# Three blocks of deformable samples gathered ahead inside the attention stage instead of two

## The chip, the cores and the metric

The kernel is one program for one NeuronCore of a Trainium2 chip; it uses one core. Time is the device time of one execution in microseconds (us). The core has five engines that each work through an instruction stream of their own, in order: TensorE (PE, matrix products and transposes), VectorE (DVE), ScalarE (ACT), GpSimd (POOL) and SyncE (SP), which here only issues transfers. Transfers run on 16 DMA engines that all queues share. The result of a transfer or an instruction is handed on by a semaphore, and an instruction that waits holds everything behind it on its engine.

## The reference, cut to what matters

The reference takes two images of 256 channels and 64 x 64 pixels through four layers:

```
x = group_norm(x) + proj(attention(group_norm(x)))      # 4 heads, 4096 x 4096 scores per head
x = x + position_term                                    # linear in the pixel's place
x = relu(x + bn(conv1x1(relu(bn(dcn(relu(bn(conv1x1(x))))))))   # bottleneck, 64 channels inside
h = relu(group_norm(x));  h = deform_conv(h, ...1)       # first deformable layer
h = relu(group_norm(h));  h = deform_conv(h, ...2)       # second
out = h + x
```

In each deformable convolution (the bottleneck's `dcn` too) every output pixel has nine taps, and every tap samples the image at a computed place: the four pixels around that place are read and weighted. In the last layer the places come from `off`: a depthwise 7 x 7 convolution followed by a 1 x 1 to 18 channels. All of it is float32.

## The kernel before, in words

**Two stages.** `attention` (line 181) computes the attention of both images, and between its steps it carries, as background work, the bottleneck of image 0 and the first part of the bottleneck of image 1. `deform` (line 1319) then runs four layers: first deformable layer of images 0 and 1, second of images 0 and 1, with image 1's bottleneck convolution beside the first of them. The order of the instructions on PE, ACT, DVE and POOL is the order in which the Python loops write them; only SP's order is chosen by the framework, which also places all the semaphores. So each loop counter below is a place in the program that can be counted without a chip.

**Attention's loop** counts score tiles with `n`, from 0 to 1024, two at a time (a pair). 256 tiles are a unit (one image, two heads), 16 tiles are a `Block` of 256 queries. A tile is 128 queries by 1024 keys: products on PE (L580), the row's largest value on DVE (L592), exponentials on ACT (L598), 16 transposes on PE (L610) that ACT and DVE copy back (L629, L627), products with the values (L639). At a block's end DVE copies the product into the one tile `o` (L471), the softmax's denominators go to DRAM and come back broadcast as `f` (`spread`, L506 and L510, both on SP), and POOL multiplies and adds them in `combine` (L519, L520, L525), four tiles into the next block.

**Background work** is a list of Python generators. `background(count)` (line 661) takes `count` steps from the first of them that has something to do. It is called with 1 once a pair, and once more for each of the pair's two tiles that has no step of its own due (from the second image on). All background products go through one PSUM tile, `pm` (pool `att_pm`, one buffer), and copies out of it are put off until the next use.

**Image 0's early samples.** When the bottleneck convolution of image 0 is done (n = 852), `early_image` (line 1197) normalizes its output, transposes it and writes it pixel by pixel into the DRAM image `img3[0]`: eight times one load, one normalized copy to `xn_d`, and two rounds of transposes, copy (L1226) and four stores (L1231). After it, `early_samples` (line 1234) computes the offsets of the first `EARLY` = 2 of 8 blocks (a block is 512 pixels, or 36 samples of 128 pixels by one tap): 14 products with the rows in the two tiles `xs` (L805), 7 shifted sums (L825), 4 selections (L839), and some fifteen small DVE operations in `corners` (line 731) that give indices and weights. Then it queues, for each sample, a gather by POOL (an indirect DMA of 128 rows of 4 KB, L848, from `img3[0]` into a staging tile) and a store by SP (L1278) of that tile into the DRAM array `samp_d`. The function `gather` inside it does one sample a call: it stores an older tile when fewer than three tiles are free, takes the oldest free tile and gathers into it. The loop calls it once a pair, and twice when n mod 16 is 10, 12 or 14, so 11 times in 16 tiles. It has three staging tiles at first; when the last block's offsets are done, five more (the two `xs`, `border` and both filter tiles) come free.

**The deformable loop** counts samples with `s`, 36 to a block, 288 to a layer, 1152 in all. At step s it gathers sample s + 8 into a `four` tile (ten buffers), ACT and DVE combine the four corners (L1489, L1495, L1504, L1508), PE transposes the result (L1526, two records a step) and multiplies it with the weights (L1545). For the first layer of image 0 and the first `EARLY` blocks, `gather` (line 1456) reads `samp_d` by a plain transfer on SP (L1466) instead of an indirect one on POOL. Offsets of later blocks run beside, through a `Side`, which takes a given number of generator steps per s; for image 0's first layer it starts at s = 14 with block 2. Image 1's bottleneck convolution (`conv`, line 1043) is another `Side`, `seconds`: 0.9 steps per s, and 2.5 more per s until s = EARLY x 36 = 72. It has 288 gathers of its own (`bfour`, also L848 on POOL), and ends at s = 135.

**Tiles.** Indices and weights of all blocks lie in the pool `bt_c` of `CORNERS` = NB + EARLY + 1 = 11 buffers. `corners` uses one work tile each for `whole` (int32) and `above` (float32). The bottleneck's `bsmp` tiles in attention have 8 buffers (`sums`).

Of the kernel before, what the change touches and what calls it, by code (L numbers as in the profile page):

```python
# [20 lines left out]
P = 128  # L21
# [4 lines left out]
K2 = 9  # L26
EPS = 1e-5
DWK = 7

EARLY = 2  # L30


GH, GW = H + 1, W + 2
# [31 lines left out]
class Net:  # L65
    def __init__(self, ctx, tc, a, out):
        self.tc, self.nc, self.a, self.out = tc, tc.nc, a, out
        nc = self.nc
        const = ctx.enter_context(tc.tile_pool(name="const", bufs=1))
        self.small = ctx.enter_context(tc.tile_pool(name="small", bufs=2))  # L70
        dram = ctx.enter_context(tc.tile_pool(name="dram", bufs=1, space=DRAM))

        self.ident = const.tile([P, P], F32, name="ident")
        make_identity(nc, self.ident)
        self.vec = const.tile([P, V_COLS], F32, name="vec")
        nc.sync.dma_start(self.vec, a["vec"])
        self.sel = const.tile([P, 32], F32, name="sel")
        self.shift = const.tile([P, DWK, 32], F32, name="shift")
        self.later = [(self.sel, a["sel"]), (self.shift, a["shift"])]

        self.img2, self.img3, self.x2d = [], [], []

        self.xn_d, self.xa_d = [], []
        for b in range(B):
            self.img2.append(dram.tile([GH * GW, 2 * CM], F32, name=f"img2_{b}"))
            self.img3.append(dram.tile([GH * GW, 2 * C], F32, name=f"img3_{b}"))
            self.x2d.append(dram.tile([C, HW], F32, name=f"x2d_{b}"))
            self.xn_d.append(dram.tile([C, HW], F32, name=f"xn_{b}"))
            self.xa_d.append(dram.tile([C, HW], F32, name=f"xa_{b}"))

        self.pos_d = dram.tile([C, HW], F32, name="pos_d")

        self.samp_d = [dram.tile([4 * K2 * P, 4 * C], F32, name=f"samp_d{i}") for i in range(EARLY)]
        self.sample = lambda: False
        self.early = {}
        self.share_d = [dram.tile([16, P], F32, name=f"share_d{n}") for n in range(2)]

        vec = self.vec
        self.bn_s = const.tile([P, 4], F32, name="bn_s")
        self.bn_t = const.tile([P, 4], F32, name="bn_t")  # L100
        rstd = self.rsqrt(vec[:, V_BNV : V_BNV + 4], 4)
        nc.vector.tensor_mul(self.bn_s, rstd, vec[:, V_BNG : V_BNG + 4])
        m = self.small.tile([P, 4], F32, name="bn_m")
        nc.vector.tensor_copy(m, vec[:, V_BNM : V_BNM + 4])

        nc.vector.tensor_sub(m[:, 1:2], m[:, 1:2], vec[:, V_DCNB : V_DCNB + 1])
        nc.vector.tensor_mul(m, m, self.bn_s)
        nc.vector.tensor_sub(self.bn_t, vec[:, V_BNB : V_BNB + 4], m)

        for v in (self.bn_s, self.bn_t):  # L110
            nc.vector.tensor_copy(v[CM:P, 0:2], v[0:CM, 0:2])
# [69 lines left out]
    def attention(self, bott):  # L181
# [5 lines left out]
        with ExitStack() as ctx:  # L187
# [489 lines left out]
            while n < last + 4 or back or more or any(own.values()):  # L677
                u, d = divmod(n, per_unit)
                if d == 0 and u < len(units):
                    plan_unit(u)  # L680
                    if u == 0:
                        back.append(prepare(1))
                    if u == 1:
                        back.append(bott.before(0, bt, ps))
                    if u == 2:
                        back.append(first_batch())
                    if u == 3:
                        back.insert(0, bott.before(1, bt, ps))
                        back.append(self.early_samples(bott, bt, held, xp, vp, kp, ps))

                def small(at):
                    steps = own.pop(at, ())
                    for f in steps:
                        f()
                    if not steps and u > 1:
                        background(1)

                if n - 1 in pts:
                    p = pts.pop(n - 1)
                    keep(n - 1, p, "ACT")  # L700
                    keep(n - 1, p, "DVE")
                ps.flush()
                sc = [scores(m) for m in (n + 2, n + 3) if m < last]
                for m in range(len(sc)):
                    lowest(n + 2 + m, sc[m])
                if n < last:
                    p = turn(e.pop(n))
                    keep(n, p, "DVE")
                if sc:
                    e[n + 2] = exponentials(n + 2, sc[0])  # L710
                if n < last:
                    keep(n, p, "ACT")

                small(n)
                if 4 <= n < last + 4:
                    attend(n - 4)
                    attend(n - 3)
                small(n + 1)
                if n < last:
                    pts[n + 1] = turn(e.pop(n + 1))  # L720
                if sc:
                    e[n + 3] = exponentials(n + 3, sc[1])
                if u or n % 8 == 0:
                    background(1)

                for _ in range(1 + (n % 16 in (10, 12, 14))):
                    more = self.sample()
                n += 2


    def corners(self, i, pt, mask, base, idx, w4, pool, w=None):
# [13 lines left out]
            nc.scalar.activation(mk, mk, AF.Exp, scale=-1.0)  # L745

        nc.vector.tensor_scalar(p, p, float(H), -1.0, ALU.min, ALU.max)
        whole = pool.tile([P, 4, K2, 2], I32, name="whole")
        nc.vector.tensor_copy(whole, p)
        yield True  # L750
        f = pool.tile([P, 4, K2, 2], F32, name="floor")
        nc.vector.tensor_copy(f, whole)
        g = pool.tile([P, 4, K2, 2], F32, name="above")
        nc.vector.tensor_tensor(g, f, p, ALU.is_gt)
        yield False
        nc.vector.tensor_tensor(f, f, g, ALU.subtract)
# [99 lines left out]
    class Bottleneck:  # L856
# [41 lines left out]
            self.od = wp.tile([P, 512], F32, name="bod")  # L898
            nc.gpsimd.memset(self.od, 0.0)

        def pools(self, ctx, gathers=5, sums=8):
            self.ahead = gathers - 1
            tc = self.net.tc
            return self.kept | {
# [292 lines left out]
    def early_image(self, bott, pools, ps):  # L1197

        nc, x2d = self.nc, self.x2d[0]
        sc, sh = self.norm_scale(bott.stats[0], bott.gmask, V_GN_G[0], V_GN_B[0], ps)  # L1200
        yield True
        v = self.img3[0].rearrange("(y x) (s c) -> y x s c", x=GW, c=C)
# [31 lines left out]
    def early_samples(self, bott, pools, held, xp, vp, kp, ps):  # L1234
# [25 lines left out]
        wide = border[:, : 8 * (W + DWK - 1)].rearrange("p (r w) -> p r w", w=W + DWK - 1)  # L1260
        nc.gpsimd.memset(wide, 0.0)
        yield True
        wf, whole = [], xs + [border]
        for cb in range(2):
            t = pools["x"].tile([P, 2, 512], F32, name="bx").rearrange("p u n -> p (u n)")
            whole.append(t)
            wf.append(t[:, : T * 2 * K2].rearrange("p (t o) -> p t o", o=2 * K2))
            self.filters(wf[cb], cb, dw, pw)
            yield True
        free = deque(x.rearrange("p u n -> p (u n)") for x in xbs)  # L1270
        gathers, stores = deque(), deque()

        def gather():
# [14 lines left out]
        for i in range(EARLY):  # L1288
# [21 lines left out]
            bott.lock = False  # L1310
            if i + 1 < EARLY:
                load(i + 1)
            if i + 1 == EARLY:
                free.extend(whole)
            for m in range(4 * K2):
                k, j = divmod(m, 4)
                gathers.append((self.samp_d[i][m * P : m * P + P, :], idx[:, j, k : k + 1]))
# [1 line left out]
    def deform(self, bott):  # L1319
# [5 lines left out]
        with ExitStack() as ctx:  # L1325
# [291 lines left out]


            last = Side(0, 1, bott.last(1, bott.kept, ps))
            seconds = Side(0, 0.9, second, lambda s: 2.5 * min(s, EARLY * BLOCK))  # L1620
            stats[0] = self.norm_stats()
            images = []
            for s in range(ALL + 16):
# [137 lines left out]
```

## Time and profile before

Six runs: 5275.01, 5289.61, 5297.96, 5290.80, 5260.32 and 5289.63 us; their median is 5289.62.

| | us |
|---|---|
| profiled execution, its own time | 5282.19 |
| its span | 5280.4 |
| attention without background of image 0's samples: n = 0 to 852 | 0 to 2454 of the span |
| early image, offsets and samples: n = 852 to 1000 | 2454 to 2947 |
| rest of attention, start of the deformable stage | 2947 to 3047 |
| deformable s = 0 to 135, beside image 1's bottleneck convolution | 3047 to 3622 |
| the rest of the deformable stage | 3622 to 5280 |

Over the whole span PE is busy 4874.8 us (92%), DVE 3943.1 (75%), ACT 3278.1 (62%) and POOL 2323.3 (44%). By the same stages:

| stretch, us | PE busy | POOL busy | granted clock of PE | DMA share | GB/s |
|---|---|---|---|---|---|
| 0 to 1452 | 1420.30 | 155.88 | 1.00 | 0.21 | 64 |
| 1452 to 2454 | 978.03 | 582.18 | 0.99 | 0.29 | 86 |
| 2454 to 2947 | 458.75 | 105.96 | 0.97 | 0.59 | 203 |
| 2947 to 3047 | 84.18 | 24.96 | 0.89 | 0.50 | 176 |
| 3047 to 3622 | 382.20 | 381.52 | 0.79 | 0.65 | 214 |
| 3622 to 5280 | 1551.30 | 1072.83 | 0.99 | 0.94 | 348 |

How to read the profile: an engine's busy time is the time in which its instructions ran, without waits and without issuing transfers. A group of instructions is given as line, engine, operation, output<-input, count, then busy time and mean duration of one, then the engine's idle time just before them and who ended it. The granted clock is the share of full clock that PE was given. The DMA share is the mean busy share of the 16 DMA engines. Some matmul records are missing from the trace (up to a few per cent), so a wait on PE whose record is missing shows as "remote".

### The profile page before, as it was taken

The page shows a single profiled execution, that of the slowest core. Times are in us where ns is not written, and L with a number is a line of the kernel's source. Part 1 is how long each engine was busy: PE and PEld are TensorE (multiplying, and loading weights), DVE is VectorE, ACT ScalarE, POOL GpSimd, SP SyncE. Part 2 cuts the span into 40 slices and gives each one's busy share as a digit, 9 for nine tenths or more (in the row PEclk, how much of TensorE's full clock was granted, in tenths as well). Part 3 has the DMA queues.
Part 4 walks back from the last instruction along what each step waited for, and adds up shares of the span by engine and source line. Part 5 has one row for each costly group of instructions (what it writes and reads, how often), then busy time and mean ns, then how long its engine had stood idle before and what let it go on. Part 6 is the DMA issues. An engine that isn't in the chain of part 4 may idle for free. (4 is left out here: it accounts for less than half of the span.)

```text
span 5280.4 us, 101084 instructions
## 1 busy us (share of the span) xinstructions
PE 4874.8 (92%) x38680; PEld 2741.5 (52%) x38680; DVE 3943.1 (75%) x7033; ACT 3278.1 (62%) x5941; POOL 2323.3 (44%) x2256
## 2 busy tenths in 40 slices
PE   8999999999999999999999856769999989999998
PEld 5555565555555555655555533434444444444444
DVE  6877767787677888687656656657778888888887
ACT  5676656666566666666656523348866666666666
POOL 0111101000026777462122267765766666666665
PEclk9999999999999999999999968889999999999999
DMA  5221111111113333232476566569989999999998
GB/s 171 60 93 59 44 61 43 49 30 45 53 52 91 98 101 93 89 89 79 139 253 244 184 235 214 181 221 340 346 319 330 366 336 343 337 394 351 350 359 312
DMA packets 367029, 997.74 MB, mean 189 GB/s; under 512 B 61373, under 2 KB 98811, under 8 KB 366543
## 3 DMA queue, kind: packets, MB, share of 16 engines
q0 software_dynamic: 196560, 690.41, 36.7%
q1 hardware_dynamic: 169438, 300.73, 17.5%
q8 instruction: 304, 4.98, 0.4%
q14 instruction: 183, 1.49, 0.1%
q10 hardware_dynamic: 544, 0.13, 0.0%
HBM read 855.36 MB, written 127.35 MB: 186 GB/s over the span
## 5 line engine op out<-in xcount | busy, mean ns | idle before, releaser
L598 ACT ACTIVATE e<-sc,low 128x1024 f32<-128x1024 f32 x1024 | 1146.3, 1119 | 717.0 <-DVE low L592 691.5
L848 POOL DMA_INDIRECT four<-img,didx x1080 | 1152.9, 1067 | 607.3 <-issue 248.9
L592 DVE TENSOR_REDUCE low<-sc 128x1 f32<-128x1024 f32 x1024 | 1204.7, 1217 | 243.9 <-PE sc L580 230.2
L1545 PE MATMUL out<-st,wc 128*128 128x512 f32 x2304 | 1219.6, 612 | 100.0 <-ACT st L1535 56.4
L639 PE MATMUL av<-et,v 128*64 128x256 f32 x8192 | 1004.4, 387 | 0.1
L580 PE MATMUL sc<-k,qs 64*128 64x512 f32 x2048 | 999.2, 606 | 2.4 <-ACT e L598 1.4
L580 PE MATMUL sc<-k,q 64*128 64x512 f32 x2048 | 980.9, 605 | 0.6 <-issue 0.3
L610 PEld LDWEIGHTS tt<-ident,e 64*128 64x128 f32 x16384 | 657.8, 139 | 545.9 <-issue 272.8
L519 POOL TENSOR_TENSOR o<-o,f 128x1024 f32<-128x1024 f32 x63 | 149.5, 2372 | 1798.0 <-DMA f<-share_d 881.9
L629 ACT COPY et<-tt 128x512 f32<-128x512 f32 x1152 | 658.4, 584 | 245.2 <-PE tt L610 178.0
L610 PE MATMUL tt<-ident,e 64*128 64x64 f32 x16384 | 734.0, 227 | 60.8 <-ACT et L629 39.1
L627 DVE COPY et<-tt 128x512 f32<-128x512 f32 x896 | 611.9, 683 | 182.1 <-PE tt L610 161.8
L639 PEld LDWEIGHTS av<-et,v 128*64 128x64 f32 x8192 | 556.1, 138 | 304.6 <-issue 52.9
L848 POOL DMA_INDIRECT bfour<-img,bidx x576 | 582.7, 1012 | 233.9 <-issue 118.0
L1495 DVE SCALAR_TENSOR_TENSOR four<-four,dwt 128x512 f32<-128x512 f32 x648 | 484.5, 748 | 253.7 <-ACT four L1489 192.9
L1514 DVE SCALAR_TENSOR_TENSOR smp<-four,dw,smp 128x256 f32<-128x256 f32 x1296 | 626.3, 483 | 51.5 <-issue 17.8
L1526 PEld LDWEIGHTS pt<-ident,smp 128*128 128x128 f32 x2304 | 329.3, 143 | 633.3 <-issue 531.6
L1545 PEld LDWEIGHTS out<-st,wc 128*128 128x128 f32 x2304 | 388.2, 195 | 356.0 <-issue 240.7
L1489 ACT ACTIVATE four<-four,dwt 128x512 f32<-128x512 f32 x648 | 465.8, 719 | 142.7 <-DMA four<-img,didx 122.9
L1535 ACT COPY st<-pt 128x1024 f32<-128x1024 f32 x288 | 289.1, 1004 | 272.4 <-PE pt L1526 178.7
L580 PEld LDWEIGHTS sc<-k,qs 64*128 64x128 f32 x2048 | 346.2, 188 | 212.4 <-issue 125.6
L1526 PE MATMUL pt<-ident,smp 128*128 128x128 f32 x2304 | 447.0, 276 | 7.0 <-issue 4.6
(194 smaller groups left out, 5003.9 us busy)
## 6 DMA issues: line engine op xcount, KB each, us to landing
f<-share_d SPq DMA_DIRECT2D x128, 256.0 KB
four<-samp_d SPq DMA_DIRECT2D x64, 512.0 KB
xb<-xn SPq DMA_DIRECT2D x55, 512.0 KB
img<-imgt SPq DMA_DIRECT2D x96, 256.0 KB
four<-img,didx POOLq DMA_INDIRECT x1080
xa<-res SPq DMA_DIRECT2D x32, 512.0 KB
samp_d<-xb SPq DMA_DIRECT2D x32, 512.0 KB
xb<-in_x SPq DMA_DIRECT2D x20, 512.0 KB
```

The costliest lines, as they stand in the source:

```text
L580: nc.tensor.matmul(s[:, j, :], lhsT=q[u, i // 2][int(h != j)][halves[j], at : at + P], rhs=k[u][c][halves[j], h, :], start=True, stop=True,)
L592: nc.vector.tensor_reduce(low, s, AX.X, ALU.max, negate=True)
L598: nc.scalar.activation(e.rearrange("p j n -> p (j n)"), s, AF.Exp, bias=blk.low[:, g, c : c + 1], accum_out=blk.sum[:, g, c : c + 1],)
L610: nc.tensor.transpose(pt[:, m, :], e[half, m // 4, m % 4 * P : m % 4 * P + P], self.ident[half, half],)
L627: nc.vector.tensor_copy(dst, pt)
L629: nc.scalar.copy(dst, pt)
L639: nc.tensor.matmul(now["av"][halves[h], :], lhsT=v[u][c][:, m, halves[h]], rhs=ets[j][:, m, h, :], start=(m == 0), stop=(m == 7),)
L848: self.nc.gpsimd.indirect_dma_start(out=dst, out_offset=None, in_=img, in_offset=bass.IndirectOffsetOnAxis(ap=idx, axis=0),)
L1495: nc.vector.scalar_tensor_tensor(uv, four[:, 2 * C :], share(s, 1, 1), uv, ALU.mult, ALU.add)
L1514: nc.vector.scalar_tensor_tensor(smps[s], four[:, c], weight(s, c), smps[s], ALU.mult, ALU.add)
L1526: nc.tensor.transpose(pts[u][:, c, j * P : (j + 1) * P], smp[:, c * P : c * P + P], self.ident,)
L1545: nc.tensor.matmul(outs[ob], lhsT=wc[k][:, c, ob * P : ob * P + P], rhs=sts[u][:, c, :], start=(k == 0 and c == 0), stop=(k == K2 - 1 and ...
```

## The change

Six edits, which belong together:

- `EARLY` is 3: block 2's offsets are computed in attention, its 36 samples are gathered and stored there (108 samples in all), and the deformable stage reads s = 0 to 107 from `samp_d` by SP. `Side` for the remaining offsets starts at s = 50 with block 3, and `CORNERS` is 12.
- `hurry`: from the start of `early_image` until block 0's offsets are done, the loop's one background call per pair takes 2 steps instead of 1. The early image then lies in n = 852 to 872 (before, to 886) and the offsets blocks end at n = 882, 888 and 896 (before, two blocks, 902 and 914).
- Samples are called for twice a pair, except once when n mod 16 is 4: 15 in 16 tiles instead of 11. Gathers run from n = 884 to 996 (before, 902 to 1004).
- Staging: three tiles until the last block's offsets are done, then two more (`border` and the second filter tile) instead of five more.
- `whole` and `above` share one work tile, and `bsmp` has 7 buffers instead of 8.
- `seconds` keeps its 2.5 more steps per s until s = 72 (2 x 36), where `EARLY` x 36 would now be 108.

```diff
-EARLY = 2
+EARLY = 3
...
+        self.hurry = 0
...
                 if u or n % 8 == 0:
-                    background(1)
+                    background(1 + self.hurry)
-                for _ in range(1 + (n % 16 in (10, 12, 14))):
+                for _ in range(2 - (n % 16 == 4)):
                     more = self.sample()
...
-        whole = pool.tile([P, 4, K2, 2], I32, name="whole")
+        whole = pool.tile([P, 4, K2, 2], F32, name="whole").bitcast(I32)
...
-        g = pool.tile([P, 4, K2, 2], F32, name="above")
+        g = whole.bitcast(F32)
...
-        def pools(self, ctx, gathers=5, sums=8):
+        def pools(self, ctx, gathers=5, sums=7):
...
     def early_image(self, bott, pools, ps):
         nc, x2d = self.nc, self.x2d[0]
+        self.hurry = 1
...
-        wf, whole = [], xs + [border]
+        wf = []
         for cb in range(2):
             t = pools["x"].tile([P, 2, 512], F32, name="bx").rearrange("p u n -> p (u n)")
-            whole.append(t)
...
-        free = deque(x.rearrange("p u n -> p (u n)") for x in xbs)
+        free, more = deque(x.rearrange("p u n -> p (u n)") for x in xbs), [border, t]
...
             if i + 1 < EARLY:
                 load(i + 1)
-            if i + 1 == EARLY:
-                free.extend(whole)
+            else:
+                free.extend(more)
+            self.hurry = 0
...
-            seconds = Side(0, 0.9, second, lambda s: 2.5 * min(s, EARLY * BLOCK))
+            seconds = Side(0, 0.9, second, lambda s: 2.5 * min(s, 2 * BLOCK))
```

## The prediction

> **What bounds the kernel now.** I read the forty slices first, then busy times by stage, then counts of one line by stage, then the POOL groups and the timeline of the stage that stood out. In the page:
>
> ```profile
> PE   8999999999999999999999856769999989999998
> POOL 0111101000026777462122267765766666666665
> PEclk9999999999999999999999968889999999999999
> ```
>
> TensorE (PE) is full except in slices 23 to 27, which are the head of the deformable stage. Busy time by stretch (columns: length, then busy time and count of PE, PEld, DVE, ACT, POOL, then granted clock, DMA share, GB/s):
>
> ```profile
> 1164.80:1338.00 173.20, 171.59 (x1882) 102.46 (x1884) 138.86 (x221) 113.46 (x213) 17.49 (x12) 1.00 0.13 38
> 2727.20:2928.20 201.00, 185.68 (x1882) 108.81 (x1884) 126.72 (x205) 122.17 (x228) 58.79 (x56) 0.94 0.70 255
> 3047.00:3456.60 409.60, 248.65 (x1032) 151.38 (x1033) 236.74 (x484) 125.85 (x223) 274.02 (x264) 0.74 0.62 201
> 3456.60:3569.00 112.40, 82.49 (x299) 43.79 (x298) 60.44 (x122) 50.83 (x89) 79.60 (x76) 0.86 0.74 237
> 3569.00:3622.00 53.00, 51.06 (x223) 27.02 (x222) 45.25 (x99) 43.16 (x77) 27.90 (x27) 1.00 0.79 268
> ```
>
> The first two rows are the same four blocks of attention (64 score tiles, n = 416 to 480 and n = 928 to 992), without and with early gathers: 43.3 and 50.25 us a block. The last three are deformable steps s = 0 to 72, 72 to 108 and 108 to 135, where image 1's bottleneck convolution runs beside image 0's first layer. The steps are counted by the transposes of L1526, two records to a step:
>
> ```profile
> 3456.60:3569.00 112.40, 14.81 (x72) 10.89 (x72) 0.86 0.74 237
> 3569.00:3622.00 53.00, 10.31 (x54) 7.58 (x54) 1.00 0.79 268
> ```
>
> So a step costs 5.69 us up to s = 72, 3.12 us up to 108 and 1.96 us up to 135. What fills the middle stage is POOL; its groups there (count | busy, mean ns | idle before, by releaser):
>
> ```profile
> L848 POOL DMA_INDIRECT four<-img,didx x40 | 42.6, 1065 | 12.5 <-issue 11.6 <-ACT smp L1504 0.6 <-DVE four L1495 0.3
> L848 POOL DMA_INDIRECT bfour<-img,bidx x36 | 37.6, 1044 | 16.9 <-issue 9.1 <-DVE bsmp L1078 6.5 <-DVE smp L1508 0.9
> ```
>
> 42.6 + 12.5 + 37.6 + 16.9 = 109.6 of 112.4 us: POOL issues gathers back to back, a `four` costing 1.065 + 0.30 = 1.37 us of its queue. In s < 72 nearly all gathers are `bfour`, and POOL stands at 274 us busy plus its 0.3 us issue gaps.
>
> In attention the early gathers come in bursts, because POOL works in order and each block's `combine` holds it until the block is done. Windows of 10 us around one burst:
>
> ```profile
> 2740.00:2750.00 10.00, 10.00 (x116) 6.09 (x114) 6.56 (x8) 6.76 (x13) 7.20 (x6) 1.00 0.23 65
> 2750.00:2760.00 10.00, 5.57 (x37) 2.30 (x33) 3.73 (x4) 2.47 (x5) 5.60 (x6) 0.83 0.98 340
> 2760.00:2770.00 10.00, 10.00 (x108) 5.99 (x110) 7.35 (x10) 6.54 (x13) 1.87 (x2) 1.00 1.03 417
> ```
>
> POOL's burst starts at 2746; PE, DVE and ACT all thin out at 2750, once, and then run on although the DMA engines stay full at 417 GB/s. The extra 7.0 us a block (50.25 less 43.3) goes with the head of the burst, not with each gather.
>
> **The change, part by part.** The emission points (n in attention, s in the deformable stage) come from running both kernels' loops. Terms are against the profiled run's own 5282.2 us, of which the span is 5280.4.
>
> a) *One more offsets block in attention.* 14 products of 126x512, 7 shifts and 4 selections, two records each. In the stretch 2440 to 2720, which holds two such blocks, L805 shows 44 + 4 + 4 + 4 records and 19.7 + 1.8 + 1.6 + 1.4 = 24.5 us, L825 3.9 us and L839 2.2 us: 30.6, or 15.3 us a block. As a check, n = 886 to 914, which held the filters and both blocks, took 105.7 us against 71.4 us for n = 374 to 402: 17 us a block. PE is full there, nothing hides it: +16 (bounds 12 to 20).
>
> b) *36 more gathers with their stores, at 15 instead of 11 a block, through five tiles instead of eight.* They run over n = 882 to 1000 instead of 902 to 1014, 7.1 blocks instead of 6.4, so there is about one more burst: +7. Bounds: per gather (27.8 us over 44 in the two rows above, 0.63 us each) 36 cost +23, and bursts that stand longer could cost more (rival 1, +52); if the head shrinks with the tiles in flight from 7 to 7 x 5/8 = 4.4 us, 7.1 x 4.4 = 31 us replace 6.4 x 7 = 45: -14. I take +7, as the timeline shows a head per burst. Does a block's work fit? The four blocks moved 51.33 MB with 87 transfers of 0.524 MB, so 1.4 MB is other traffic; 15 gathers and 15 stores make 15.7 + 1.4 = 17.1 MB, which at the 417 GB/s of the last row is 41 us of a 50 us block. POOL: 11 or 12 gathers are emitted between one combine and the next block's `spread`, so the stores ahead of `f<-share_d` on SP should have gone out some 10 us before it is due.
>
> For this the Trainium skill has a rule that speaks against the change: "DMA: Bandwidth & Descriptors", Specifications, gives an HBM limit of about 358 GB/s per core. By it 17.1 MB would take 48 us, all but the whole block, and the sum would hold rival 1's +52 in place of b's +7. This trace has 417 GB/s in windows that only move gathers and stores, so here the sum does not use the page's limit.
>
> c) *Image at two background steps.* It takes n = 852 to 872 instead of 886, with the same instructions: 16 rounds of transposes through the one `pm` bank, copy, four stores. Before, 118.7 us for 34 n against some 92 at 43.3 a block: 27 us, mostly PE's own. Squeezed, the bank and two `bx` tiles turn round faster; while the image is written the DMA share already reaches 0.94 in a 10 us window. If each of the 16 rounds waited for one more copy (L1226, 0.69 us) it would be 11, and 20 with a late `bx` load or two; spread over fewer pairs it may also lose less: +3 (bounds -5 to +20).
>
> d) *Two loads of `xs` rows now stand behind sample stores on SP* (before, the one such load stood ahead of all of them), and PE takes them in order: +3 (bounds 0 to +20, from the 21.0 us that the 4 MB load `x<-xn` takes on the chain).
>
> e) *36 gathers leave POOL in the deformable stage*: s = 72 to 108 reads `samp_d` through SP. Without them POOL has about 0.9 `bfour` a step there, so the steps should fall to those just behind, which have the same convolution rate and an offsets block beside: 36 x (3.12 - 1.96) = 42 us; and s = 64 to 72, when 8 of these were issued into a full queue, 8 x 1.37 = 11. Some of both is one saving, and the 36 at issue cost are 49: -50 (bounds -26, rival 2, to -53). SP's 36 more loads are issued eight steps ahead and move the same bytes.
>
> f) *Offsets block 2 leaves s = 19 to 55*: 28 records of 0.593 us are 16.6 us of PE, but PE is 61% busy in that stage and POOL decides. DVE waited 12.9 us once for its `pos`. -8 (bounds 0 to -17).
>
> g) *At nothing*: merging `whole` and `above` (same engine, same order), seven `bsmp` tiles for eight (a tile is read two steps before it is wanted again), a longer `corner` pool, and the conv rate 2.5 up to s = 72, which is what it was. If the seven tiles bound, POOL would wait on PE in the first convolution, off PE's path.
>
> Sum: 16 + 7 + 3 + 3 - 50 - 8 = -29: 5253 us on the profiled run's scale. That run lies 7.4 us under the median of the six (5289.6), so 5260.6, say 5260.
>
> **Rivals.**
> 1. *The transfers bind attention* (slower). If a block's 17.1 MB ran at the 348 GB/s that 3622 to 5280 holds at a DMA share of 0.94, it would need 49 us, and POOL stands a further 4.4 us in `combine` and 3 to 4 us for `f`: 57 us a block, 13.7 over the bare 43.3, for 7.1 blocks: 97 us where the bursts cost 45 now, so +52 in place of b's +7: net +16, and +50 with c and d at their ends. It decides from a block of about 58 us. For it: PE already loses 7 us a block. Against: 417 GB/s in the saturated windows. About 5310 to 5340.
> 2. *POOL was not the only bound of s = 72 to 108.* In that stage ACT waits 27.1 us in three pieces for the convolution's transposes and DVE 28.3 us on ACT; if the 27 remain, e saves 53 - 27 = 26, and the net is -5: 5285.
> 3. *The burst's head shrinks with five tiles*: b at -14 rather than +7, net -50: 5240.
> That the early work does not finish in time is out: in the loops the last of 108 stores falls at n = 1000, of 1028.
>
> **How the numbers follow.** This kernel's runs spread from 5260 to 5298; about 0.5%, 26 us, is what can be told from no change. Chances: forecast 0.45 (net -50 to -12, so 5240 to 5278: about 0.33 beyond -26 and 0.12 within), rival 1 0.18 (0.16 beyond +26), rival 2 0.22 (0.20 within, 0.02 slower), rival 3 0.15 (all beyond -26). Together faster 0.48, same 0.33, slower 0.19. The range goes from rival 3 with e and f at their far ends (-50 - 3 - 9 = -62: 5228) to the lower part of rival 1 (5316).
>
> **What would show it.** Right: attention ends 25 to 35 us later, blocks with samples near 50 us with one dip of PE each, PE full in n = 874 to 896; s = 72 to 108 in 70 to 80 us, with POOL mostly idle, s = 0 to 72 near 400. Wrong: blocks of 55 us and more with `combine` waiting for `f` or for stores (rival 1); ACT still waiting on the convolution at s = 72 to 108 and a stage over 95 us (rival 2); PE waits on `bx` or `xs` loads between n = 852 and 896 (c and d at their ends).

## The result, and the profile after

The changed kernel takes 5324.18 us (median of 20 runs, 5305.18 to 5341.41); the kernel before, run beside it, 5282.24 (46 runs, 5260.32 to 5303.89). The ratio is 1.0079, with a 95% interval of 1.0068 to 1.0090: the change costs 42 us, where a gain of 29 was forecast. The profiled execution after took 5341.25 us (span 5339.4), 17 us above its median, so single stages are compared below with some care.

Counted by the same loop steps, the two profiled executions part like this:

| stage | before, us | after, us | difference | forecast |
|---|---|---|---|---|
| attention, n = 0 to 852 | 2454 | 2453 | -1 | 0 |
| attention, n = 852 to 1023 | 562.0 | 647.3 | +85 | +29 |
| deformable, s = 0 to 72 | 409.7 | 399.8 | -10 | -19 |
| s = 72 to 108 | 112.2 | 69.9 | -42 | -42 |
| s = 108 to 135 | 53.3 | 63.7 | +10 | 0 |
| s = 135 to the end | 1658 | 1674 | +16 | 0 |

The forecasts of the deformable stage are the parts of e and f as they were worked out, 3 us more than the sum took for them.

The deformable stage gave most of what was asked of it. Attention took back twice that. The forty slices of the page after:

```profile
PE   8999999999999999998987756588999999999998
...
POOL 0111110000027776461132246765666566666665
```

Slices 21 to 23, 2670 to 3070 us, are the blocks of attention with samples. PE was at 9, 9, 8 there before and is at 8, 7, 7 now, while POOL is not busier than 2 to 4 tenths: no engine has taken over what PE lost. The hole in slices 24 to 27 (5, 6, 5, 8) is the old one (5, 6, 7, 6), shorter at its end.

Busy time by stretch, after, for the same steps as before: n = 416 to 480, n = 928 to 992, s = 0 to 72, 72 to 108, 108 to 135 (length, then PE, PEld, DVE, ACT, POOL, clock, DMA share, GB/s):

```profile
1163.30:1336.20 172.90, 171.39 (x1882) 102.34 (x1884) 138.81 (x221) 113.44 (x213) 17.48 (x12) 1.00 0.14 38
2759.60:3000.30 240.70, 181.70 (x1867) 107.35 (x1864) 126.91 (x205) 122.00 (x228) 72.68 (x71) 0.89 0.80 286
3131.70:3531.50 399.80, 235.75 (x983) 145.24 (x984) 232.83 (x468) 124.37 (x219) 266.38 (x255) 0.73 0.64 208
3531.50:3601.40 69.90, 68.88 (x300) 37.41 (x299) 61.51 (x127) 51.17 (x91) 48.88 (x44) 1.00 0.92 328
3601.40:3665.10 63.70, 53.66 (x223) 28.11 (x222) 45.93 (x100) 43.88 (x77) 36.22 (x34) 0.92 0.80 271
```

The first row, four blocks without samples, is unchanged at 43.2 us a block. The second, four blocks with samples, went from 50.25 to 60.2 us a block, though PE did no more work in it (181.70 us, before 185.68). The DMA engines are *less* than full there, 0.80 and 286 GB/s, although their bytes are what the change added. In the fourth row PE is busy 68.88 of 69.90 us: POOL's bound is gone from s = 72 to 108, and PE is what is left. The transposes of L1528 (L1526 before), two records to a step, place the steps:

```profile
3531.50:3601.40 69.90, 13.75 (x73) 10.13 (x73) 1.00 0.92 328
3601.40:3665.10 63.70, 10.78 (x54) 7.93 (x54) 0.92 0.80 271
```

1.94 us a step up to s = 108, where it was 3.12. POOL's groups in that stage (count | busy, mean ns | idle before, by releaser):

```profile
L849 POOL DMA_INDIRECT bfour<-img,bidx x35 | 39.8, 1138 | 18.6 <-DVE bsmp L1079 7.1 <-issue 6.4 <-DMA four<-samp_d 1.7
L849 POOL DMA_INDIRECT four<-img,didx x9 | 10.5, 1167 | 2.7 <-issue 2.1 <-DVE smp L1510 0.3 <-DMA four<-img,didx 0.3
```

Nine gathers of `four` instead of 40, as the loops say.

**Where attention loses it.** Ten-us windows of the block at 2830 to 2870, the same columns:

```profile
2830.00:2840.00 10.00, 10.00 (x102) 5.51 (x100) 5.65 (x8) 7.28 (x14) 0.94 (x1) 1.00 0.98 383
2840.00:2850.00 10.00, 6.63 (x69) 4.19 (x65) 2.79 (x3) 3.39 (x7) 0.00 (x0) 1.00 0.49 158
2850.00:2860.00 10.00, 1.36 (x17) 1.22 (x19) 2.86 (x6) 0.28 (x1) 6.49 (x6) 0.52 0.60 147
2860.00:2870.00 10.00, 10.00 (x94) 5.82 (x92) 7.87 (x21) 6.96 (x14) 2.73 (x4) 0.80 0.96 338
```

Before, the dip of PE fell together with DMA engines that were full. Now PE, ACT and POOL stop while the DMA engines drop to half. So look for what all wait for. The waits of n = 928 to 992 (engine, line, who ended the wait: us in total, times, longest), after:

```profile
POOL xb L849 <- DMA samp_d<-xb: 72.3, 22, 7.2
POOL o L520 <- DMA f<-share_d: 70.4, 4, 20.4
DVE o L472 <- POOL avs L526: 62.6, 4, 20.0
PE tt L611 <- DVE et L628: 54.7, 4, 18.4
```

In the kernel before, no wait of DVE at this copy (L471 there) ends with POOL in these blocks. Lines 2 to 4 are one chain, once a block: `combine` waits for `f`, the product copy into `o` waits for `combine`, the copy `et` stands behind it on DVE, and PE waits for `et`: 54.7 us in four blocks, 13.7 a block. What makes `f` late is to be read on SP, whose timeline after has (start, length, queue, line, transfer):

```profile
2823.85 8.24 SPq L1279 DMA_DIRECT2D samp_d<-xb  x3
2833.96 0.32 SPq L1279 DMA_DIRECT2D samp_d<-k  x1
2835.48 0.32 SPq L1279 DMA_DIRECT2D samp_d<-bx  x1
2838.13 0.32 SPq L1279 DMA_DIRECT2D samp_d<-xb  x1
2838.54 0.39 SPq L558 DMA_DIRECT2D xa<-res  x1
2843.69 0.37 SPq L215 DMA_DIRECT2D res<-xa  x1
2844.16 0.42 SPq L507 DMA_DIRECT2D share_d<-shares  x1
...
2847.57 1.10 SPq L511 DMA_DIRECT2D f<-share_d  x2
```

and POOL and DVE, around the same time:

```profile
2823.05 0.27 DVE L505 COPY shares<-pm 16x128 f32<-16x128 f32 x1
...
2842.11 0.68 DVE L628 COPY et<-tt 128x512 f32<-128x512 f32 x1
2857.11 0.42 DVE L472 COPY o<-av 128x256 f32<-128x256 f32 x1 [14.31 <-POOL avs L526]
```

```profile
2831.26 0.94 POOL L849 DMA_INDIRECT xb<-img,bidx  x1 [2.83 <-DMA samp_d<-xb]
2852.60 2.34 POOL L520 TENSOR_TENSOR o<-o,f 128x1024 f32<-128x1024 f32 x1 [20.40 <-DMA f<-share_d]
```

The shares are ready at 2823.3. SP could send them at once, but six sample stores stand ahead, each waiting for its own gather to land, and then a store and a load of attention's rows. `share_d` goes out at 2844.2, 20.8 us late. Its store, the load of `f` and `combine` then follow one after the other until 2857.1, and all that time no gather starts, because the next block's gathers stand behind `combine` on POOL. In the kernel before, DVE and SP at the like place:

```profile
2733.57 0.27 DVE L504 COPY shares<-pm 16x128 f32<-16x128 f32 x1
2733.87 0.32 SPq L506 DMA_DIRECT2D share_d<-shares  x1
2737.01 1.11 SPq L510 DMA_DIRECT2D f<-share_d  x2
```

There the shares were ready at 2733.8, and `share_d` left within 0.1 us, as in all blocks with samples of this execution.

### The profile page after: what moved, and what is told of

It is laid out like the page before. It is cut to its first block, busy times and chain, and to the rows that moved or that the text cites. A ratio compares the mean times of both kernels' runs of the same rounds, so it can differ in the third digit from the quotient of the medians.

```text
span 5339.4 us, 101269 instructions
## 1 busy us (share of the span) xinstructions
PE 4876.3 (91%) x38680; PEld 2739.0 (51%) x38680; DVE 3942.9 (74%) x7033; ACT 3278.5 (61%) x5941; POOL 2319.9 (43%) x2256
## 5 line engine op out<-in xcount | busy, mean ns | idle before, releaser
L849 POOL DMA_INDIRECT four<-img,didx x1044 | 1111.7, 1065 | 615.9 <-issue 242.0
L1528 PEld LDWEIGHTS pt<-ident,smp 128*128 128x128 f32 x2304 | 330.9, 144 | 632.0 <-issue 527.4
L1497 DVE SCALAR_TENSOR_TENSOR four<-four,dwt 128x512 f32<-128x512 f32 x612 | 457.6, 748 | 230.2 <-ACT four L1491 182.8
L1491 ACT ACTIVATE four<-four,dwt 128x512 f32<-128x512 f32 x612 | 439.6, 718 | 126.0 <-DMA four<-img,didx 103.2
L1528 PE MATMUL pt<-ident,smp 128*128 128x128 f32 x2304 | 448.6, 277 | 1.2 <-DVE smp L1510 0.8
```

The lines of the kernel that those rows point to most:

```text
L849: self.nc.gpsimd.indirect_dma_start(out=dst, out_offset=None, in_=img, in_offset=bass.IndirectOffsetOnAxis(ap=idx, axis=0),)
L1497: nc.vector.scalar_tensor_tensor(uv, four[:, 2 * C :], share(s, 1, 1), uv, ALU.mult, ALU.add)
L1528: nc.tensor.transpose(pts[u][:, c, j * P : (j + 1) * P], smp[:, c * P : c * P + P], self.ident,)
```

## The experiments

Theories: **Q**, SP's order: the shares stand behind the block's sample stores, so `combine` is late, and through it PE. **R**, the transfers' rate binds, and a late `f` is only its symptom (rival 1 of the prediction). **T**, the five staging tiles set the pace. **P**, POOL's order alone makes `combine` late. **S**, it is the number of samples that costs, not their pace. **R2**, once SP is free, what still costs is that the DMA engines are nearly full.

The twelve runs were made on another occasion than the result, in three lots of four. The kernel before took 5107.71, 5105.01 and 5106.52 us in them, some 3% less than in the result, so each kernel is given as a ratio to the kernel before of its own lot. "Block" is a quarter of n = 928 to 992; "late" is the time from the shares' copy on DVE to `share_d` on SP; "attention" is n = 852 to 1023.

| kernel | ratio, 95% | block, us | late, us, blocks with samples | attention, us |
|---|---|---|---|---|
| a0, the changed kernel | 1.0144 [1.0128, 1.0161] | 60.6 | 19 to 23 | 647.7 |
| e4, deformable half alone | 0.9923 [0.9906, 0.9940] | 44.8 | 0 to 9 | 530.0 |
| e8, before at 15 samples in 16 tiles | 1.0086 [1.0069, 1.0103] | 56.0 | 10 to 18 | 568.6 |
| e2, eight staging tiles | 1.0090 [1.0073, 1.0107] | 56.2 | 14 to 20 | 624.2 |
| e3, no hurry | 1.0098 [1.0081, 1.0115] | 57.9 | 9 to 24 | 630.7 |
| e1, shares and f from ACT's queue | 1.0138 [1.0121, 1.0155] | 55.3 | not SP's | 628.0 |
| e6, 13 samples with a gap | 1.0107 [1.0090, 1.0124] | 54.5 | 11 to 23 | 628.8 |
| e5, no factors | 0.9977 [0.9968, 0.9987] | 46.0 | | 562.7 |
| e7, stores from POOL's queue | 1.0018 [1.0008, 1.0027] | 48.8 | 0 | 580.3 |
| e9, the same at 13 | 0.9979 [0.9966, 0.9991] | 45.6 | 0 | 558.1 |
| e10, the same at 12 | 1.0012 [1.0003, 1.0022] | 45.9 | 0, last block 19 | 562.7 |
| e11, before with stores from POOL's queue | 0.9987 [0.9977, 0.9996] | 44.1 | 0 | 521.1 |

**a0: the changed kernel again**, no edit.

> The changed kernel itself, on the same chip as the three experiments beside it. All theories: a ratio to the kernel before of about 1.008 to 1.014; blocks of attention with samples (n = 928 to 992) 55 to 60 us each, the first product of combine idle behind f for about 20 us a block, the product copy into o idle behind combine for 14 to 20 us a block.

1.0144, 5178.96 us. The row of n = 928 to 992 and its waits repeat those of the result:

```profile
2736.55:2979.02 242.47, 181.74 (x1882) 108.15 (x1884) 126.99 (x205) 121.83 (x229) 73.32 (x73) 0.87 0.81 286
...
POOL o L520 <- DMA f<-share_d: 72.2, 4, 20.1
DVE o L472 <- POOL avs L526: 67.7, 4, 18.9
```

The change costs 74 us on this occasion. Attention is 118 us longer than in e4, which has the attention of the kernel before.

**e1: the shares and `f` on ACT's queue.**

```diff
+                    due(at + 17, self.shares)
+                    due(at + 18, self.factors)
...
-                    nc.sync.dma_start(d, t)
+                    nc.scalar.dma_start(self.share_d[self.i % 2], self.t)
...
-                        nc.sync.dma_start(
+                        nc.scalar.dma_start(
```

> The changed kernel with share_d and f issued from ACT's queue, one and two steps after the transposition, instead of SP's; nothing else differs. Theory Q (SP's order: share_d and f stand behind 15 sample stores, each of which waits for its gather, so POOL's combine and with it DVE's copy into o come 13 to 20 us late in every block): the blocks with samples fall from 60 us to 50 to 52, n = 928 to 992 from 240.7 us to 200 to 210, and the time from 5324 to 5255 to 5275, 0.995 to 0.999 of the kernel before. Theory R (the transfers' rate: 15 samples at 340 to 390 GB/s and the serial part after them fill 57 us or more whatever the queue): blocks stay at 57 us or more, time 5305 to 5325, and DVE's wait for POOL at o stays over 10 us a block.

1.0138, no better than a0. Attention was 20 us shorter than in a0, and about as much was lost elsewhere: 5 us ahead of n = 852, 9 between attention's last exponentials and the first transposes of the deformable stage, 7 in s = 0 to 72. The run did not take `f` out of SP's line, as its timeline of ACT shows:

```profile
2810.85 5.63 ACTq L518 DMA_DIRECT2D f<-share_d  x2
2816.53 0.60 ACT L288 ACTIVATE q<-pm 128x512 f32<-128x512 f32 x1 [13.40 <-DMA res<-xa]
```

By the records, `f`'s first half was released at 2810.7 by a sample store of SP and its second at 2816.0 by SP's load of `res`. Neither writes anything that `f` reads. In the built program the transfers of SP's and ACT's queues take turns on the same eight completion semaphores, and `f` waits on those whose last users were these two. So ACT, and with it the exponentials, now stood behind SP's stores too. That the run lost as much as a0 says nothing for R.

**e2: eight staging tiles.**

```diff
-        wf = []
+        wf, more = [], xs + [border]
...
+            more.append(t)
...
-        free, more = deque(x.rearrange("p u n -> p (u n)") for x in xbs), [border, t]
+        free = deque(x.rearrange("p u n -> p (u n)") for x in xbs)
```

> The changed kernel with all eight staging tiles again once the last block's offsets are done (both xs, border and both filter tiles come free instead of border and one filter tile). Theory T (five tiles make the chain gather, land, store, land of a sample set the pace, 3.2 us a sample, and so the backlog on SP): with eight the pace is the transfers' 2.5 us, 15 stores are out in 38 us, blocks fall to 50 to 53 us, time 5265 to 5285. Theory Q: the stores ahead of share_d are the same 15; part of the backlog may go, blocks 55 to 60, time 5300 to 5325. Theory R: no change, 5315 to 5330.

1.0090: 0.0054 less than a0, some 28 us (give or take 12, by the two intervals), of the 118 in question. The chain stays whole:

```profile
POOL o L520 <- DMA f<-share_d: 85.6, 4, 24.0
```

T is a part, a quarter, and not the cause.

**e3: no hurry.** `self.hurry = 1` becomes 0, nothing else.

> The changed kernel with one background step per pair throughout (hurry stays 0): the image lies in n = 852 to 886 again and the samples begin some 16 tiles later, still inside attention. If squeezing the image costs what the traces suggest (94.9 us for image and filters against about 87 for the same work spread out), the time falls by about 8, to 5316; by the price of the prediction (3) to 5321; if the late x and xs loads of the squeezed image were most of the loss, by 20 or more, to 5304 or less.

1.0098, 0.0046 or 23 us less than a0, as uncertain as in e2. The image itself is not where this lies: of n = 852 to 872 in e9, 83.0 us, and 852 to 886 in e4, 118.1 us, the fourteen more tiles of e4 are 14 x 43.3 / 16 = 37.9, and 83.0 - (118.1 - 37.9) = +2.8 us for the image in fewer pairs. The `f` of seven blocks is still 9 to 24 us late. Where the other 20 us go was not followed.

**e4: the deformable half alone.** The kernel before; blocks 0 to 2 of the first layer are read from `samp_d`, where block 2 reads block 1's samples with block 1's weights. It leaves out block 2's offsets and its 36 gathers, in both stages.

```diff
-            corners = {(0, 0, i): (None, None, w) for i, w in self.early.items()}
+            corners = {(0, 0, i): (None, None, self.early[min(i, 1)]) for i in range(3)}
...
-                    if n == 0 and i < EARLY:
+                    if n == 0 and i < 3:
...
-            offs = [Side(EARLY * BLOCK - LEAD - 6, OFFS / BLOCK, begun)]
+            offs = [Side(3 * BLOCK - LEAD - 6, OFFS / BLOCK, begun)]
```

> The kernel before with the deformable half of the change alone: block 2 of image 0's first layer is read from samp_d by SP, its offsets are not computed there, the later offsets start at s = 50. The attention half is left out: block 2 is given block 1's samples and weights again, so block 2's offsets and samples are not computed anywhere. By the prediction this half is worth 58 us (5282 - 58 = 5224, 0.989). By the trace of the changed kernel (s = 0 to 135 shorter by 42 us) it is 5240, 0.992. If what came off POOL is given back later in the layer (s = 108 on was 10 to 25 us longer there), 5250 to 5265, 0.994 to 0.997.

0.9923, which is -39.4 us, where 58 were summed for this half. s = 72 to 108 takes 72.5 us, against 112.5 in e11 and 114.5 in e8, which have the old deformable stage: -40 to -42, as forecast. s = 0 to 72 takes 341.0 against 344.5 and 345.5: -4 where -19 was forecast.

**e5: no factors.** From n = 880 on `spread` does nothing, and `combine` uses the last `f` loaded before: the softmax denominators of the last nine blocks are left out.

```diff
                 def spread(self):
+                    if 16 * self.i + self.u * per_unit >= 880:
+                        self.f = Block.kept
+                        return
...
+                    Block.kept = self.f
```

> Leaves out, from n = 880 on, the softmax denominators: no transpose of the shares, no share_d, no f; combine multiplies with the last f that was loaded before (so the last nine blocks of attention are not divided rightly). All gathers, stores and products stay. Theory Q (f stands on SP's queue behind the block's sample stores, so combine comes late and DVE's product copy holds PE): combine no longer waits for a transfer, the blocks at n = 928 to 992 fall from 55-60 to 50-52 us, attention from n = 896 to 1023 is 40 to 60 us shorter than in the changed kernel and the ratio to the kernel before falls to 0.998-1.003. Theory R (the transfers' rate binds, f is late only as a symptom): blocks stay at 55 us or more, ratio above 1.006. Theory P (POOL reaches combine late by itself, behind 15 gathers that wait for tiles): combine's own wait goes, the product copy's wait for combine stays above 10 us a block, and blocks stay above 54 us.

0.9977, and attention is 85 us shorter than in a0. All gathers, stores and products are there. The row of n = 928 to 992, and its two waits on POOL's work:

```profile
2725.22:2909.33 184.11, 176.37 (x1878) 105.00 (x1880) 125.45 (x201) 121.39 (x229) 72.41 (x72) 0.98 0.98 358
...
POOL xb L852 <- DMA samp_d<-xb: 93.0, 25, 12.3
...
DVE o L472 <- POOL avs L529: 9.6, 2, 5.3
```

POOL still waits 93 us for staging tiles, more than in a0, but the wait for `f` is gone and DVE's fell from 67.7 to 9.6 us. Blocks take 46.0 us and the DMA engines run at 0.98: the same work goes through once nothing stands still. Q, and better than Q's 50 to 52; R and P fall.

**e6: 13 samples, with a gap ahead of `spread`.**

```diff
-                for _ in range(2 - (n % 16 == 4)):
+                for _ in range({12: 1, 14: 0}.get(n % 16, 2)):
```

> 13 samples in 16 tiles instead of 15, with the pause put just ahead of spread: one at n mod 16 = 12, none at 14. The samples end about n = 1017 instead of 996. Theory Q: the stores that stand ahead of share_d at the block's end fall from about five to about one or two, f is late by under 8 us, blocks 50-53 us, and though samples run for 8.3 blocks instead of 7.2 the ratio falls to 0.996-1.004. Theory R: the bytes of 13 samples still take 13/15 of the time, so blocks fall in proportion only to 51-53 us, but f stays late by 12 us or more and there are more blocks: ratio 1.003-1.010. The two differ in the wait of combine for f.

1.0107; blocks 54.5 us. A miss for Q's numbers: `share_d` is still 11 to 18 us late in all but the last of these blocks, and

```profile
POOL o L520 <- DMA f<-share_d: 70.4, 4, 19.4
```

A gap in the order of emission is not a gap on SP. The stores go out as their gathers land, and a block's gathers start only when the late `combine` is done, so thirteen stores fill SP's line up to the shares nearly as fifteen do. By its wait for `f` alone this run fitted R as well as Q; e5 and e7 part them.

**e7: the stores on POOL's queue.** Nothing is left out.

```diff
-                nc.sync.dma_start(dst, four)
+                nc.gpsimd.dma_start(dst, four)
```

> The samples' stores are issued from POOL's queue instead of SP's; nothing is left out. SP then holds only share_d, f and the attention's own loads. Theory Q: share_d goes out within 1 us of the shares, f is there when POOL comes to combine, combine's wait for f falls from 20 to under 5 us, blocks fall to 50-53 us, ratio 0.997-1.004, unless POOL itself, which now waits in order for each gather before its store, comes to combine 10 us or more late. Theory R: the same bytes at the same rate, blocks stay at 55 us or more, ratio above 1.006. Theory P (POOL's order is what is late): f is on time and blocks are as long as before or longer, ratio 1.008-1.020, with the product copy waiting for combine and combine waiting for nothing.

1.0018: one word gives back 64 us of 74. The row of n = 928 to 992, two waits, and POOL's group of `combine`'s first product:

```profile
2724.62:2919.80 195.18, 176.89 (x1882) 105.58 (x1884) 126.03 (x205) 121.52 (x229) 108.84 (x132) 0.96 0.97 351
...
POOL samp_d L1279 <- DMA xb<-img,bidx: 31.4, 31, 2.9
DVE o L472 <- POOL avs L526: 24.7, 4, 10.4
...
L520 POOL TENSOR_TENSOR o<-o,f 128x1024 f32<-128x1024 f32 x4 | 9.5, 2368 | 0.1
```

`share_d` goes out with the shares, and `combine` waits 0.1 us instead of 72. Part of P appears now: POOL waits in order for gathers before their stores, so `combine` itself comes 18 to 20 us after the shares, and DVE waits 24.7 us in four blocks. Blocks are 48.8 us against 60.6.

**e8: the kernel before at 15 samples in 16 tiles.** One part of the change alone, with eight tiles and two blocks.

```diff
-                for _ in range(1 + (n % 16 in (10, 12, 14))):
+                for _ in range(2 - (n % 16 == 4)):
```

> The kernel before with one part of the change alone: samples called for 15 times in 16 tiles instead of 11. Two blocks of samples, 72 gathers, eight staging tiles, no hurry. Theory Q: 15 stores stand ahead of share_d, it goes out 12 to 20 us after the shares, blocks with samples take 54 to 58 us for about 4.8 blocks, where 11 in 16 take 44.75 us for 6.5 blocks (the run with the deformable half alone). 4.8 x (56 - 43.3) - 6.5 x 1.5 = +51 us: ratio 1.007 to 1.012, with nothing gained for it. Rival S (it is the number of samples, not their pace, that costs: the same 72 samples cost the same): ratio 0.998 to 1.003.

1.0086, Q's figure. The same 72 samples cost 44 us more when they are called for faster, so S falls; and

```profile
POOL o L519 <- DMA f<-share_d: 91.1, 4, 27.8
```

The pace alone makes the wait: neither the third block nor the missing tiles are needed for it.

**e9 and e10: stores on POOL's queue, 13 and 12 samples in 16 tiles.**

```diff
-                for _ in range(2 - (n % 16 == 4)):
+                for _ in range(2 - (n % 16 in (4, 10, 14))):
```

In e10 the list is (2, 6, 10, 14).

> The changed kernel with the stores on POOL's queue, and 13 samples in 16 tiles instead of 15 (one where n mod 16 is 4, 10 or 14); nothing left out. Theory R2 (with the queue mended, the DMA engines at 0.97 busy are what still costs): a block's bytes fall by 13/15, the DMA share to 0.85-0.93, blocks from 48.8 to 45-47.5 us; over 8.3 instead of 7.2 blocks 8.3 x 3 - 7.2 x 5.5 = -15 us: ratio 0.996 to 1.001. Theory P (POOL waits in order for each gather before its store, and combine comes late by that): blocks 47.5 us or more, ratio 1.001 to 1.004.

> As the run with 13, with 12 samples in 16 tiles (one where n mod 16 is 2, 6, 10 or 14). The samples end at n = 1028, with the last tile of attention. Theory R2: DMA share 0.80-0.88, blocks 44-46 us, 9 x 2 - 7.2 x 5.5 = -22 us against 15 in 16: ratio 0.995 to 0.999, unless the last samples stand in the way of the deformable stage's first loads (the time from the last exponential of attention to the first transpose of the deformable stage grows over 33 us). Theory P: blocks 47 us or more, ratio 1.000 to 1.004.

e9: 0.9979, 12.8 us under the kernel before, and the fastest kernel here that leaves nothing out. Its row and waits of n = 928 to 992:

```profile
2723.16:2905.64 182.48, 174.38 (x1882) 104.62 (x1884) 126.51 (x205) 121.51 (x229) 96.65 (x116) 0.98 0.93 331
...
POOL o L520 <- DMA f<-share_d: 18.4, 4, 6.0
...
DVE o L472 <- POOL avs L526: 11.8, 4, 5.5
```

R2's block (45 to 47.5) and DMA share (0.85 to 0.93). e10 is no faster within attention, and loses after it: from attention's last exponentials to the first transposes of the deformable stage it takes 58.8 us, against 30.9 in e9. The exception in its expectation came true, through SP once more. The last lines of SP's timeline in e10:

```profile
3021.47 0.37 SPq L912 DMA_DIRECT2D bx<-xa  x1
3021.89 0.46 SPq L507 DMA_DIRECT2D share_d<-shares  x1
...
3027.24 1.13 SPq L511 DMA_DIRECT2D f<-share_d  x2
```

The load `bx<-xa` of the bottleneck had stood at the head of SP's queue since 2995.4, waiting for sample stores to land, the last of which went out at 3017.5 and landed at 3021.0; `bx` is one of the staging tiles. The last block's shares, ready at 3002.9, stood behind it.

**e11: the kernel before with its stores on POOL's queue**, the edit of e7 in the kernel before.

> The kernel before with its sample stores issued from POOL's queue instead of SP's; nothing else. Theory Q: at 11 stores a block share_d is late by only 5 to 9 us (the run with the deformable half alone), which the four tiles between spread and combine nearly cover, so little is to be had: blocks 44 to 45 us, ratio 0.996 to 1.001. Rival P (POOL's own waits for gathers push combine back): ratio 1.002 to 1.008. If it is well below 0.996, the queue cost the kernel before something too.

0.9987, or 5 us; attention 521.1 us against 530.0 in e4. At 11 stores a block the shares were 5 to 9 us late in five of e4's blocks, and most of that was covered by the four tiles between `spread` and `combine`.

## Why the prediction was wrong

**a, the offsets block: right.** PE's three groups in 2440 to 2720, after:

```profile
L806 PE MATMUL pm<-v,bx 128*126 128x512 f32 (+3 forms) x84 | 35.6, 581 | 0.0
L826 PE MATMUL pm<-k,shift 126*32 126x512 f32 x42 | 5.9, 602 | 0.3 <-DVE res L556 0.2
L840 PE MATMUL pm<-sel,bst 128*128 128x32 f32 x24 | 3.2, 279 | 0.8 <-ACT bst L835 0.8
```

44.7 us for three blocks, 14.9 a block, where 15.3 was read from two and 16 entered. This is PE's own work.

**b, the gathers: wrong, and most of the miss.** It was entered at +7 (-14 to +52). Of the 85 us that attention lost in the result, 15 are a and 3 are c, and about 67 are left for b and d; on the other occasion 118 - 18 = 100. The step that failed is the sentence "the stores ahead of `f<-share_d` on SP should have gone out some 10 us before it is due". It counted the emissions between one `combine` and the next `spread`, and forgot that a store is not done with SP when it is emitted: it waits at the head of SP's queue for its gather to land, about 3 us a sample here. Fifteen samples last from 2794.9, when the first gather after `combine` starts, to 2838.1, when the last store goes out: 43 us of a block whose bare length is 43. So `share_d` was 16 to 23 us late instead of 10 us early, and that is a loop: a late `f` makes a late `combine`, behind which the next block's gathers start late. e5 and e7 break it at two different places and take 85 and 67 us out of attention; e8 makes it in the kernel before by the pace alone. With SP free, b is still not the +7 of the sum: at the changed kernel's pace (e7) attention's 580.3 us less e4's 530.0 and less a and c leave 50 - 18 = 32 us, with the DMA engines at 0.97 and DVE waiting 6 us a block for `combine`. At 13 in 16 (e9) 28 - 18 = 10 us are left; against e11, which has the same queue for its stores, it is 37 - 18 = 19. So SP's order is about two thirds of what b cost, and the pace of 15 most of the rest. The forecast had priced the samples as if SP were free.

**Rival 1** had the right signs, blocks of 58 us and more with `combine` waiting for `f`, and the wrong cause. Its own number speaks against it: the transfers ran at 286 GB/s and 0.80 while attention lost most, and at 358 GB/s and 0.98 when the wait was taken away. Its time, 5310 to 5340, holds the 5324 that came, but by another cause, and its price of +52 for b was below the 67 and 100. The two are told apart by looking at whether the DMA engines are full in the dips of PE: they are at 0.49 and 0.60 in the block shown above.

**The 417 GB/s.** That figure was from windows of 10 us; the check that a block's work fits used it for whole blocks, 41 us for 17.1 MB. With nothing in the way a stretch of 184 us held 358 GB/s (e5) and one of 195 us 351 GB/s (e7). The Trainium skill, "DMA: Bandwidth & Descriptors", Specifications, gives about 358 GB/s for a core, and the prediction set that aside; it is what the saturated stage sustained here. By it, as an estimate, a block needs 48 us, and e7's blocks take 48.8. So the page's figure was the better one for a stage, though it is not what made the changed kernel slow; whether it is this limit that held e5 and e7, no run shows.

**c and d.** The image cost +2.8 us for the forecast +3. Of d nothing is seen: from n = 872 to 896 of the profile after (2536.2 to 2656.1) PE is busy 114.4 of 119.9 us, and none of its waits there ends with a load. The hurry as a whole costs about 23 us in the changed kernel (e3 against a0), with the late `f` in both.

**e and f: the right mechanism, one size off.** s = 72 to 108 fell by 42 us as forecast, to 1.94 us a step, and PE is full there. Rival 2, in which ACT's wait for the convolution would have held the stage at 95 us or more, is out. But s = 0 to 72 fell by 10 us in the result and by 4 in e4, where the 11 us for the full queue at s = 64 to 72 and the 8 us of f were added. The half alone is worth 39 us instead of 58 (e4), and which of the two terms was too large was not tried. The 26 us that the result lost after s = 108, where nothing was forecast, did not come again: 61.7 and 1590 us in a0 against 63.4 and 1593 in e11. Their cause is open.

**Rival 3**, the burst's head shrinking with five tiles, was wrong in its sign: eight tiles instead of five save about 28 us (e2).

**g** held as far as the profile shows it: POOL does not wait on `bsmp` in the attention's rows, and in s = 72 to 108 its wait on `bsmp` L1079 is 7.1 us, off PE's path.

Put together, on the second occasion: +15 for a, +3 for c, about +100 for the samples (what is left of the 118), -39 for the deformable half, +79 against +74 measured.

Two slips in the prediction's figures changed nothing: the 7.1 and 6.4 blocks go with the gathers' own ends (n = 884 to 996 and 902 to 1004, which make 7.0 and 6.4), not with the n named beside them, and the chances given by outcome add up to 0.34 for the same and 0.18 for slower, not 0.33 and 0.19.

## What to carry to other kernels

An in-order queue that only issues transfers has a critical path of its own: a small, urgent transfer behind many patient ones, each of which waits for another transfer to land, is as late as the last of them (here 16 to 23 us), however idle the issuing engine looks; ask of every queue what stands ahead of the urgent item and when each of those can *leave*, not when it was emitted. Where the engines stand still in the same 10 us in which the DMA engines are far from full (here 0.49 and 0.60), look for such an order before bandwidth. Here moving the patient stores to the queue that already issued their gathers, and slowing them from 15 to 13 in 16 tiles, turned +1.4% into -0.2%.

## What the hardware showed beyond that

- Two queues of plain transfers were not independent here. In e1 `f` on ACT's queue was released by a store and a load of SP's that it has nothing to do with, and ACT stood still for 13.40 us. Moving the *other* party, the stores, to POOL's queue set SP free (e7: 0 us late).
- The kernel before took 5282 us on one occasion and 5105 to 5108 on another. Of 175 us, the deformable steps s = 0 to 72 are some 65 (409.7 us against 344.5 in e11, whose deformable stage is the same), and s = 135 to the end another 65 (1658 against 1593). On the first occasion its blocks with samples took 50.25 us with dips of PE whose cause no recorded wait shows, though `share_d` was on time; on the second they take 44.8 (e4). The cause of the difference was not tried, and the 7 us a block in the prediction stay unexplained.
- The changed kernel lost more on the second occasion: 74 us against 42. The difference is in the kernel before: its attention from n = 852 on took 562 us on the first occasion and 530 on the second (e4), while the changed kernel's took 647 and 648. Blocks that the chain of waits sets were as long on both, 60.2 and 60.6 us.
